# Layer 0 of a four-layer image network: how q*v is stored and how the right-hand blocks are loaded

## The chip, the cores and the metric

One core of one Trainium2 chip runs the whole network, in float32. The metric is the device time of one execution in microseconds (us). Before the change it is 5754.43 us, the median of three runs (5752.62 to 5759.0).

## What is computed

The input is 8 images of 56 x 56 pixels and 192 channels. Four layers follow one another, each as `x = x + layer(group_norm(x))`. The change lies in layer 0 alone. Cut to what matters, that layer is:

```python
p = silu(x @ p_w.T + p_b); q = silu(x @ q_w.T + q_b); v = silu(x @ v_w.T + v_b)   # 192 -> 576 channels
a1 = rpe_mlp(positions, t1) * decay      # for each channel, one coefficient for each of 111 lags
a2 = rpe_mlp(positions, t2) * decay
qv = q * v                               # (8, 56, 56, 576)
o1 = toeplitz(qv, a1)  # along a row:    o1[h, w] = sum over w' of a1[w - w'] * qv[h, w']
o2 = toeplitz(qv, a2)  # along a column: o2[h, w] = sum over h' of a2[h - h'] * qv[h', w]
out = (p * (o1 + o2)) @ o_w.T + o_b
```

For one channel, `o1 + o2` is a product of matrices, qv (56 x 56) times a Toeplitz matrix, plus another Toeplitz matrix times qv. The kernel makes one product of it: the left operand has the 56 rows of a Toeplitz matrix and the 56 rows of qv above one another in its partitions, the right operand has qv and the other Toeplitz matrix in the same order, and TensorE sums over all these partitions.

## The kernel before

Layer 0 has two stages, written one after the other from line 1320 on.

**The q*v stage** (lines 1322 to 1361) loops over the 8 images. `layer0_load` (353) fetches an image into `x0` by a transfer that GpSimd (POOL) issues. An image lies as 128 partitions, 64 channels of each half of the pixels, by 3 groups of channels by 1568 pixels (`NH`). `layer0_in` (358) takes the statistics on VectorE (DVE) at line 157 and normalizes into `xn0` on DVE at line 371, for image 0 in four pieces of 392 pixels (`TT`) and for the others in one instruction. `layer0_qv` (374) walks over the image in 14 tiles (`PH`) of 112 pixels, two image rows of each half. For each tile and each half `n` of the 576 channels TensorE (PE) does 24 matmuls at line 387, DVE adds the bias from PSUM into `act` (line 393, four buffers), ScalarE (ACT) applies SiLU in place (394), and DVE multiplies q by v into `qv` (395). The sync engine (SP) stores the tile twice: to `left`, where a row of 56 x 64 values is one image row h, with one transfer for each half of the pixels (398), and to `right`, where a row is one image column w, with two transfers for each half (403). All these stores move pieces of 256 B.

Between the tiles, lists of other steps are worked off (`between`, line 1341): `toeplitz_rows` (227) makes the coefficients and stores the Toeplitz rows to `left` and `right` from ACT's queue, 64 rows for each group of 64 channels, of which 56 hold coefficients (`row`, 295) and 8 hold zeros (`zeros`, 300). `build_bias_mask` (307) and `layer1_weights` (624) prepare layer 1; their transfers are issued by POOL.

**The mix stage** (`layer0_mix`, 523) goes through each image in three passes (`PASSES`, line 27), over nine groups of 64 channels: four, four and one. `layer0_block` (410) loads one group into two tiles of 128 partitions by 3584 values, `lt` from `left` and `rt` from `right`, with two buffers each. One transfer fills one tile: of `lt` the even partitions with a Toeplitz row and the odd ones with a row of qv, of `rt` the other way round, 64 rows of each, so the partitions past the 56th pair meet zero rows. `layer0_operand` (422) copies eight channels at a time into matmul operands, `lc` on POOL and `rc` on DVE and ACT in turn (line 425); `layer0_products` (428) multiplies them on TensorE (433) and the result is copied out (590, 593). While the products of one pass run, the gate of the pass before it (`layer0_gate`, 435, and `layer0_gate_last`, 477) is worked off in pieces. After the first pass the image before is stored to `x1` by two transfers of 64 partitions (`store`, 536), the image is normalized again (531) and the next one loaded (`load`, 526). All transfers of the mix stage go out from SP, in one order.

In both stages the order in which each engine and each queue gets its instructions is made by the framework's scheduler; no order is written out by hand there. Each engine works its instructions off in that order, so one that waits holds up all behind it.

Of the kernel before, what the change touches and what calls it, by code (L numbers as in the profile page):

```python
# [10 lines left out]
F32 = mybir.dt.float32  # L11
AF = mybir.ActivationFunctionType
# [6 lines left out]
NT = H * W  # L19
# [43 lines left out]
NH = NT // 2  # L63
NTH = NH // TT
# [25 lines left out]
def kernel(ctx: ExitStack, tc: tile.TileContext, a: dict, out: bass.AP):  # L90
# [45 lines left out]
    none = dram.tile([QR], F32, name="none")  # L136
    left, right = (dram.tile([(nimg * W + 64) * NSUB, QR], F32, name=n) for n in ("left", "right"))
    qv_row = lambda b, s: (b * NSUB + s) * W
    toep_row = lambda s: nimg * NSUB * W + 64 * s
# [87 lines left out]
    def toeplitz_rows(psum, pool, rows):  # L227
# [62 lines left out]
        zero = pool.tile([128, QR // 128], F32, name="zero", bufs=1)  # L290
        nc.gpsimd.memset(zero, 0.0)
        nc.scalar.dma_start(none.rearrange("(p n) -> p n", p=128), zero)
        parts = [z[toep_row(0):].rearrange("(s k) n -> k s n", k=64) for z in (left, right)]
# [6 lines left out]
        def zeros(i, k):  # L300
            nc.scalar.dma_start(parts[i][k], none.partition_broadcast(NSUB))

        rows += [lambda i=i, k=k: zeros(i, k) for i in range(2) for k in range(W, 64)]
# [54 lines left out]
    def layer0_in(b, x, pool, psum):  # L358

        sc, sh = scsh[:, 0, b:b + 1], scsh[:, 1, b:b + 1]  # L360
        st = pool.tile([128, 3, NTH, 6], F32, name="gh_st")
        for t in range(NTH):
            gn_piece(st, x, t)
        mv = pool.tile([128, 1, 2], F32, name="gh_mv")
        gn_aggregate(st, mv[:, 0])
        run(gn_finish(mv, sc, sh, pool, psum, "qv"))
        xn = pool.tile([128, 3, NH], F32, name="xn0")
        n = NH if b else TT
        for t in range(NH // n):
            ts = bass.ts(t, n)  # L370
            nc.vector.tensor_scalar(xn[:, :, ts], x[:, :, ts], sc, sh, ALU.mult, ALU.add)
        return xn

    def layer0_qv(b, xn, pool, psum, w_qv, b_qv, between):

        lv, rv = (
            z[qv_row(b, 0):qv_row(b, 0) + NSUB * W].rearrange("(s h) (w d) -> s h w d", h=W, d=64) for z in (left, right)
        )
        for i in range(PH):
            qv = pool.tile([2 * W, 2, D1], F32, name="qv", bufs=3)  # L380
            for n in range(2):
                ns = slice(n * D1 // 2, (n + 1) * D1 // 2)
                ps = [psum.tile([2 * W, 2, 512], F32, name=f"qv{s}", tag="qv") for s in range(2)]
                for which in range(2):
                    for j in range(3):
                        for s in range(2):
                            nc.tensor.matmul(  # L387
                                ps[s][:, which, 0:D1 // 2], xn[64 * s:64 * s + 64, j, bass.ts(i, 2 * W)],
                                w_qv[64 * s:64 * s + 64, j, which, ns], start=(j == 0), stop=(j == 2),
                            )  # L390
                for s in range(2):
                    act = pool.tile([2 * W, 2, D1 // 2], F32, name="act", bufs=4)
                    nc.vector.tensor_tensor(act, ps[s][:, :, 0:D1 // 2], b_qv[:, :, ns], ALU.add)  # L393
                    nc.scalar.activation(act, act, AF.Silu)  # L394
                    nc.vector.tensor_tensor(qv[:, s, ns], act[:, 0], act[:, 1], ALU.mult)
            for s in range(2):
                h0 = H // 2 * s + 2 * i
                nc.sync.dma_start(
                    lv[:, h0:h0 + 2].rearrange("s h w d -> (h w) s d"),
                    qv[:, s].rearrange("t (s d) -> t s d", d=64),  # L400
                )
                for r in range(2):
                    nc.sync.dma_start(
                        rv[:, :, h0 + r].rearrange("s w d -> w s d"),
                        qv[r * W:(r + 1) * W, s].rearrange("w (s d) -> w s d", d=64),
                    )
            for step in between[i]:
                step()

    def layer0_block(b, s, raws):  # L410
# [3 lines left out]
        rows_qv, rows_t = qv_row(b, s), toep_row(s)  # L414
        for t, z, even, odd in ((raw[0], left, rows_t, rows_qv), (raw[1], right, rows_qv, rows_t)):
            one = z[even:even + 64]
            nc.sync.dma_start(
                t, bass.AP(one.tensor, one.offset, [[QR, 64], [(odd - even) * QR, 2], [1, QR]]),
            )
        return raw  # L420

    def layer0_operand(copy, raw, name, bufs, d0, nu, pool):

        c = pool.tile([128, 2, 8, W], F32, name=name, bufs=bufs)
        copy(c[:, 0:nu], raw.rearrange("p (w u d) -> p u d w", u=nu, d=64 // nu)[:, :, d0:d0 + 8])  # L425
# [896 lines left out]
    with ExitStack() as st:  # L1322
# [3 lines left out]
        b_qv = pool.tile([2 * W, 2, D1], F32, name="b_qv", bufs=1)  # L1326
        nc.scalar.dma_start(b_qv.rearrange("p a d -> p (a d)"), a["b_qv"].partition_broadcast(2 * W))
# [11 lines left out]
        for b in range(nimg):  # L1339

            between = {i: [lambda i=i: pop(rows, 2 if i % 3 == 1 else 1)] for i in range(PH)}
            if b == 0:
                for i in range(PH):
# [340 lines left out]
```

## Time and profile before

| | us |
|---|---|
| median of three runs | 5754.43 |
| the profiled execution, its time | 5770.6 |
| the profiled execution, its span | 5768.8 |
| q*v stage, from the first line-387 matmul to the first products | 28 to 850 |
| mix stage | 850 to 2041 |
| TensorE busy in these two | 731 of 822 and 1072 of 1191 |
| DVE busy in these two | 601 of 822 and 646 of 1191 |
| POOL busy in these two | 45 of 822 and 550 of 1191 |
| DMA share in these two | 0.85 and 0.67 |

Times in the profile are measured from the start of the span. PE is TensorE's matmul, PEld its weight load, SPq, ACTq and POOLq are the instructions with which an engine issues transfers. The DMA share is the mean busy share of the 16 DMA engines. "Idle before, releaser" in a group's line is the time that the engine stood still just ahead of these instructions, and what it then waited for. After layer 0 come three more layers, to 5768.8 us, whose code is the same in both kernels.

### The profile page before, as it was taken

The numbers are of one execution on the slowest core, as the hardware profiler recorded it, in microseconds if no ns is written. First come the engines' busy times: TensorE is split into PE (matmuls) and PEld (weight loads), VectorE is DVE, ScalarE is ACT, GpSimd is POOL, SyncE is SP. The second block draws the span as 40 slices with busy tenths as digits, with TensorE's granted clock in tenths as the row PEclk, the third lists the DMA queues.
The fourth block names the chain that finished last, engine by engine and source line by source line (L and its number), as shares of the span: only waits on it lengthen the run. The fifth ranks groups of instructions, "written<-read, shape, count | busy, mean of one in ns | idle before, by whom it ended". The sixth has DMA issues, their size and how long they took to land. (4 is left out here: it accounts for less than half of the span.)

```text
span 5768.8 us, 116138 instructions
## 1 busy us (share of the span) xinstructions
PE 5181.2 (90%) x50342; PEld 3376.1 (59%) x50342; DVE 3336.5 (58%) x4710; ACT 2169.1 (38%) x2908; POOL 1420.2 (25%) x1107
## 2 busy tenths in 40 slices
PE   6898998999899979999997989999788798999999
PEld 4568765666666645555554657676344597444444
DVE  5777774555555546566665868888778202433331
ACT  2333443333333423333332004555476400433333
POOL 2100004444444424433342013333101101100100
PEclk8999999999999989999998989999899899999999
DMA  6888986776677633222222866666687598212211
GB/s 179 204 211 216 206 182 258 264 264 258 247 262 264 222 92 82 69 75 76 69 65 76 260 235 218 227 232 209 160 232 215 222 328 295 78 62 77 76 41 26
DMA packets 721922, 1013.94 MB, mean 176 GB/s; under 512 B 486376, under 2 KB 645444, under 8 KB 694644
## 3 DMA queue, kind: packets, MB, share of 16 engines
q1 hardware_dynamic: 706352, 940.12, 52.4%
q0 software_dynamic: 8512, 40.62, 2.1%
q10 hardware_dynamic: 6548, 25.78, 1.4%
q8 instruction: 396, 6.49, 0.5%
q14 instruction: 114, 0.93, 0.0%
HBM read 676.92 MB, written 345.97 MB: 177 GB/s over the span
## 5 line engine op out<-in xcount | busy, mean ns | idle before, releaser
L387 PE MATMUL qv<-w_qv_sb,xn 64*112 64x288 f32 x5376 | 711.3, 421 | 48.6 <-DVE act L393 45.4
L425 POOL COPY lc<-lt 128x896 f32<-128x896 f32 (+1 forms) x320 | 552.5, 1751 | 640.9 <-PE op L433 543.1
L387 PEld LDWEIGHTS qv<-w_qv_sb,xn 64*112 64x112 f32 x5376 | 558.5, 182 | 195.5 <-DVE act L393 58.1
L394 ACT ACTIVATE act<-act 112x576 f32<-112x576 f32 x448 | 300.6, 683 | 466.8 <-DVE act L393 427.4
L433 PE MATMUL op<-rc,lc 128*56 128x56 f32 x9216 | 339.1, 221 | 102.1 <-POOL lc L425 64.9
L433 PEld LDWEIGHTS op<-rc,lc 128*56 128x56 f32 x9216 | 307.8, 135 | 177.9 <-POOL lc L425 103.5
L1289 PE MATMUL ph<-y,w_sb 64*128 64x392 f32 x2304 | 397.7, 497 | 6.5 <-ACT hid L1293 6.5
L1300 PE MATMUL po<-hid,w_sb 128*64 128x392 f32 x2304 | 386.3, 494 | 0.0
L393 DVE TENSOR_TENSOR act<-qv,b_qv 112x576 f32<-112x576 f32 x448 | 320.7, 752 | 92.7 <-PE qv L387 92.4
L1307 DVE TENSOR_TENSOR x<-x,z 128x392 f32<-128x392 f32 x96 | 67.0, 698 | 524.2 <-ACT z L1305 524.2
L425 ACT COPY rc<-rt 128x896 f32<-128x896 f32 (+1 forms) x160 | 256.3, 1606 | 249.7 <-PE op L433 227.2
L805 PE MATMUL qk_ps<-xr,wg 64*96 64x392 f32 x1536 | 334.2, 538 | 1.8 <-DVE xr L752 1.7
L1016 PE MATMUL cv<-zc,wt 128*128 128x224 f32 x1536 | 313.6, 356 | 24.2 <-DMA zc<-pd 24.2
L1016 PEld LDWEIGHTS cv<-zc,wt 128*128 128x128 f32 x1536 | 291.0, 190 | 67.5 <-issue 51.2
L1289 PEld LDWEIGHTS ph<-y,w_sb 64*128 64x128 f32 x2304 | 220.0, 188 | 175.9 <-issue 25.5
L445 PE MATMUL pj<-xn,w_p_sb 64*128 64x392 f32 x1536 | 309.8, 511 | 12.4 <-DVE xn L533 8.2
L1190 PE MATMUL cps<-zc,wt 128*128 128x224 f32 x1536 | 300.2, 356 | 18.2 <-DMA zc<-zd 16.8
L1190 PEld LDWEIGHTS cps<-zc,wt 128*128 128x128 f32 x1536 | 289.6, 189 | 28.7 <-issue 21.3
L466 PE MATMUL y<-pp,w_o_sb 128*64 128x392 f32 x1536 | 285.9, 501 | 4.8 <-DVE x L474 4.1
L459 DVE TENSOR_TENSOR pp<-pp,ot 128x784 f32<-128x784 f32 x128 | 124.2, 970 | 284.8 <-ACT pp L450 272.9
L1300 PEld LDWEIGHTS po<-hid,w_sb 128*64 128x64 f32 x2304 | 162.7, 137 | 213.8 <-issue 213.8
L1031 POOL TENSOR_TENSOR rows<-rows,loc 128x896 f32<-128x896 f32 x96 | 220.8, 2300 | 261.7 <-ACT rows L1027 201.9
(233 smaller groups left out, 8895.1 us busy)
## 6 DMA issues: line engine op xcount, KB each, us to landing
lt<-left SPq DMA_DIRECT2D x72, 1792.0 KB
rt<-right SPq DMA_DIRECT2D x72, 1792.0 KB
left<-qv SPq DMA_DIRECT2D x224, 252.0 KB
right<-qv SPq DMA_DIRECT2D x448, 126.0 KB
wt<-in_band_dram SPq DMA_DIRECT2D x23, 2048.0 KB
wt<-in_band_dram SPq DMA_DIRECT2D x11, 4096.0 KB
zc<-pd SPq DMA_DIRECT2D x187, 232.0 KB
pd<-pt SPq DMA_DIRECT2D x7, 5568.0 KB
```

The costliest lines, as they stand in the source:

```text
L387: nc.tensor.matmul(ps[s][:, which, 0:D1 // 2], xn[64 * s:64 * s + 64, j, bass.ts(i, 2 * W)], w_qv[64 * s:64 * s + 64, j, which, ns], start ...
L393: nc.vector.tensor_tensor(act, ps[s][:, :, 0:D1 // 2], b_qv[:, :, ns], ALU.add)
L394: nc.scalar.activation(act, act, AF.Silu)
L425: copy(c[:, 0:nu], raw.rearrange("p (w u d) -> p u d w", u=nu, d=64 // nu)[:, :, d0:d0 + 8])
L433: nc.tensor.matmul(op[64 * u:64 * u + W, i, :], lc[:, u, i], rc[:, u, i], start=True, stop=True)
L445: nc.tensor.matmul(ps[0:M, s, 0:TT], w_p[64 * s:64 * s + 64, j, d0:d0 + M], xn[64 * s:64 * s + 64, j, ts], start=(j == 0), stop=(j == 2),)
L466: nc.tensor.matmul(y[64 * s:64 * s + 64], w_o[0:M, c, 64 * j:64 * j + 64], pp[0:M, s], start=(c == gated[0][0]), stop=(c == gated[-1][0]),)
L805: nc.tensor.matmul(in_pairs(ps[s]), wg[64 * s:64 * s + 64, j, c0:c0 + HC], in_slots(xr[64 * s:64 * s + 64], (3 * g + j) * GW), start=(j == ...
L1016: nc.tensor.matmul(dst, wt[:, c4 + i, 128 * q:128 * q + 128], zc[:, :, c4 + i, q:q + NPAIR], start=(q == 0), stop=(q == 1),)
L1190: nc.tensor.matmul(dst.rearrange("p (b n) -> p b n", n=NPAIR), wt[:, c4 + i, q * OP:(q + 1) * OP], zc[:, :, c4 + i, q:q + NPAIR], start=(q ...
L1289: nc.tensor.matmul(ps[:, s, 0:TT], w0[64 * s:64 * s + 64, j, m * 128:(m + 1) * 128], y[64 * s:64 * s + 64, j, ts], start=(j == 0), stop=(j ...
L1300: nc.tensor.matmul(ps[64 * s:64 * s + 64], w1[:, m, 64 * j:64 * j + 64], hid[:, m, s], start=(m == 0), stop=(m == 5),)
```

## The change

- Images 0, 2, 4 and 6 store q*v once, to `left` alone. Their tiles need no longer end on an image row: they are 13, twelve of 120 pixels and one of 128 (`QT`). Images 1, 3, 5 and 7 keep 14 tiles of 112 pixels and both stores. `right` holds q*v of the odd images only.
- For an even image the q*v half of `rt` is gathered from `left`: partition w gets, for each h, the 64 channels at (h, w), in pieces of 256 B.
- A block is loaded without zero rows, by four transfers of 56 rows: partitions 0 to 55 and 56 to 111 of `lt`, and the same of `rt`. The copies at line 425 and the products work on 112 partitions instead of 128. The zero rows are no longer written.
- In the q*v stage the product q times v is made on DVE for the first half of the pixels and on POOL for the second.
- Normalizing in the q*v stage is done in four pieces for every image, on DVE for image 0 and on POOL for the others.

```diff
+QT = [[(120 * i, 120) for i in range(12)] + [(1440, 128)], [(112 * i, 112) for i in range(14)]]
...
-    none = dram.tile([QR], F32, name="none")
-    left, right = (dram.tile([(nimg * W + 64) * NSUB, QR], F32, name=n) for n in ("left", "right"))
+    left, right = (dram.tile([n * NSUB, QR], F32, name=z) for n, z in ((nimg * W + 64, "left"), (nimg // 2 * W + 64, "right")))
     qv_row = lambda b, s: (b * NSUB + s) * W
-    toep_row = lambda s: nimg * NSUB * W + 64 * s
+    toep_row, right_row = (lambda s, n=n: n * NSUB * W + 64 * s for n in (nimg, nimg // 2))
...
-        rows += [lambda i=i, k=k: zeros(i, k) for i in range(2) for k in range(W, 64)]
         rows += [lambda i=i, w0=w0: row(i, w0) for i in range(2) for w0 in range(W)]
...
-        n = NH if b else TT
-        for t in range(NH // n):
-            ts = bass.ts(t, n)
-            nc.vector.tensor_scalar(xn[:, :, ts], x[:, :, ts], sc, sh, ALU.mult, ALU.add)
+        for t in range(NTH):
+            ts = bass.ts(t, TT)
+            eng = nc.gpsimd if b else nc.vector
+            eng.tensor_scalar(xn[:, :, ts], x[:, :, ts], sc, sh, ALU.mult, ALU.add)
...
-        for i in range(PH):
-            qv = pool.tile([2 * W, 2, D1], F32, name="qv", bufs=3)
+        for i, (t0, M) in enumerate(QT[b % 2]):
+            qv = pool.tile([128, 2, D1], F32, name="qv", bufs=3)
...
-                    nc.vector.tensor_tensor(qv[:, s, ns], act[:, 0], act[:, 1], ALU.mult)
+                    eng = (nc.vector, nc.gpsimd)[s]
+                    eng.tensor_tensor(qv[0:M, s, ns], act[0:M, 0], act[0:M, 1], ALU.mult)
...
                 nc.sync.dma_start(
-                    lv[:, h0:h0 + 2].rearrange("s h w d -> (h w) s d"),
-                    qv[:, s].rearrange("t (s d) -> t s d", d=64),
+                    bass.AP(one.tensor, one.offset + 64 * (NH * s + t0), [[64, M], [64 * NT, NSUB], [1, 64]]),
+                    qv[0:M, s].rearrange("t (s d) -> t s d", d=64),
                 )
-                for r in range(2):
+                for r in range(2 * (b % 2)):
                     nc.sync.dma_start(
-                        rv[:, :, h0 + r].rearrange("s w d -> w s d"),
+                        rv[:, :, H // 2 * s + 2 * i + r].rearrange("s w d -> w s d"),
                         qv[r * W:(r + 1) * W, s].rearrange("w (s d) -> w s d", d=64),
                     )
...
-        rows_qv, rows_t = qv_row(b, s), toep_row(s)
-        for t, z, even, odd in ((raw[0], left, rows_t, rows_qv), (raw[1], right, rows_qv, rows_t)):
-            one = z[even:even + 64]
+        x, at = left[qv_row(b, s):qv_row(b, s) + W], qv_row(b // 2, s)
+        nc.sync.dma_start(raw[0][0:W], left[toep_row(s):toep_row(s) + W])
+        nc.sync.dma_start(raw[0][W:2 * W], x)
+        nc.sync.dma_start(raw[1][W:2 * W], right[right_row(s):right_row(s) + W])
+        if b % 2:
+            nc.sync.dma_start(raw[1][0:W], right[at:at + W])
+        else:
             nc.sync.dma_start(
-                t, bass.AP(one.tensor, one.offset, [[QR, 64], [(odd - even) * QR, 2], [1, QR]]),
+                raw[1][0:W].rearrange("w (h d) -> w h d", d=64), x.rearrange("h (w d) -> w h d", d=64)
             )
...
-        c = pool.tile([128, 2, 8, W], F32, name=name, bufs=bufs)
-        copy(c[:, 0:nu], raw.rearrange("p (w u d) -> p u d w", u=nu, d=64 // nu)[:, :, d0:d0 + 8])
+        c = pool.tile([2 * W, 2, 8, W], F32, name=name, bufs=bufs)
+        copy(c[:, 0:nu], raw[0:2 * W].rearrange("p (w u d) -> p u d w", u=nu, d=64 // nu)[:, :, d0:d0 + 8])
```

The bias `b_qv` is loaded for 128 partitions instead of 112, and the loops over `between` run over as many tiles as the image has.

## The prediction

> **What bounds the kernel now.** I read the page first, for which engine is busy where, then the busy times by stretch over layer 0, then the sync queue's order of issue and the waits. Layer 0 has two stages. The q*v stage (line 387) runs from 28 to 850 us of the span, the mix stage (lines 410 to 621) from there to 2041 us.
>
> ```profile
> span 5768.8 us, 116138 instructions
> L387 PE MATMUL qv<-w_qv_sb,xn 64*112 64x288 f32 x5376 | 711.3, 421 | 48.6 <-DVE act L393 45.4
> L425 POOL COPY lc<-lt 128x896 f32<-128x896 f32 (+1 forms) x320 | 552.5, 1751 | 640.9 <-PE op L433 543.1
> ```
>
> In the q*v stage TensorE is busy 711.3 of 822 us with its own line alone: TensorE sets that stage. In the mix stage it is not so even. One image takes 149 us there. The columns below are: stretch, then busy us and instructions of PE, PEld, DVE, ACT, POOL, then granted clock, DMA share, GB/s.
>
> ```profile
> 1150.00:1210.00 60.00, 50.68 (x891) 33.36 (x890) 42.64 (x52) 25.79 (x25) 38.48 (x19) 0.97 0.78 265
> 1210.00:1251.00 41.00, 37.76 (x540) 25.69 (x540) 19.17 (x24) 17.66 (x17) 21.12 (x12) 1.00 0.87 360
> 1251.00:1299.00 48.00, 48.00 (x458) 31.63 (x455) 21.49 (x31) 15.07 (x17) 9.69 (x9) 1.00 0.40 154
> ...
> 1307.00:1411.00 104.00, 91.52 (x1456) 63.23 (x1454) 62.48 (x77) 44.52 (x43) 60.34 (x33) 0.98 0.88 330
> ```
>
> Each image has three passes. In the first two the DMA share is 0.78 and 0.87 and TensorE has gaps; in the third (1251:1299) TensorE is full and the DMA engines are half idle. The next image's blocks 2 to 8 and one further all fall into 1307:1411. The sync queue shows that the transfers pace this:
>
> ```profile
> 1376.90 0.51 SPq L417 DMA_DIRECT2D lt<-left  x1
> ...
> 1388.20 0.51 SPq L417 DMA_DIRECT2D lt<-left  x1
> ...
> 1399.15 0.51 SPq L417 DMA_DIRECT2D lt<-left  x1
> ```
>
> A block (lt and rt, 3.67 MB) every 11 us is what 330 GB/s gives. With two buffers each, a third pair can't be loaded ahead, so a slower block load shows in the time. Price of a block now: from the first issue of that stretch (1307.0) to the issue of the eighth (1399.2) lie seven blocks, the x1 store (2.41 MB at 203 GB/s, row below, 11.9 us) and the x load (2.41 MB at 424, 5.7): (92.2 - 17.6) / 7 = 10.7 us.
>
> The rows that the change turns on are transfers that touch only half of the partitions:
>
> ```profile
> 1044.00:1049.00 5.00, 4.35 (x76) 3.18 (x74) 4.62 (x6) 2.96 (x3) 4.85 (x3) 1.00 0.95 203
> 1050.00:1052.00 2.00, 2.00 (x19) 1.26 (x16) 0.00 (x0) 0.35 (x2) 1.83 (x2) 1.00 0.98 204
> 1061.00:1064.00 3.00, 2.84 (x26) 1.83 (x23) 0.97 (x1) 0.65 (x2) 2.95 (x2) 1.00 1.05 445
> ```
>
> The first two are the x1 store of line 538, two transfers of 64 partitions: all DMA engines are busy, and move 203 GB/s. The third is the x load of line 528, 128 partitions: 445 GB/s at 1.05, so 424 at full share. Half of the partitions, half of the pace; and the second half of the store (1050:1052), though it is queued behind the first, doesn't make it up by running beside it.
>
> **The change, part by part.**
>
> *Block loads in four transfers of 56 rows.* Removed: 72 x 2 transfers of 128 rows. Added: 72 x 4 of 56 rows, into partitions 0:56 or 56:112, so each lies nearly in one half. Bytes fall from 3.67 to 3.21 MB. The nearest row for the pace is the 203 GB/s of the x1 store. By bytes a transfer of 56 x 14336 B = 0.803 MB takes 3.95 us; but rows move whole (the stretch from 1376 to 1411 has 791 large packets for 11.3 MB, one row of 14336 B each), and 56 rows over 16 engines leave four rows on the busiest, as 64 rows do, which is 0.918 MB at 203, 4.52 us. Four transfers: 15.8 to 18.1 us. I take 17.0, between them, because engines with three rows start on the next transfer. The far bound is that nothing is lost: 3.21 MB at 330 GB/s, 9.7 us. [...]
>
> *Gathered right-hand blocks, images 0, 2, 4, 6.* One of the four transfers becomes 56 x 56 pieces of 256 B. No 256 B read is in the trace of before; the nearest row is the 256 B stores of the q*v stage, where reading and writing change places:
>
> ```profile
> 775.00:825.00 50.00, 50.00 (x416) 37.12 (x414) 40.29 (x70) 23.23 (x35) 0.00 (x0) 1.00 0.88 181
> ...
> q1 hardware_dynamic: 35708, 8.95, 87.6%
> ```
>
> 0.876 x 16 x 50 us / 35708 = 19.6 ns a piece on an engine, so 3136 pieces over 16 take 3.8 us. Upper bound: half pace again, 7.7 us. I take 4.2, near the lower end, since 256 B in 19.6 ns is 13 GB/s an engine, what the half-partition rows reach anyway (203 / 16). With three plain transfers (12.8) an even block also comes to 17.0 us; its bounds are 7.3 + 3.8 = 11.1 and 13.6 + 7.7 = 21.3.
>
> *Sum of the mix stage.* Seven blocks of an image wait in that chain: 7 x (17.0 - 10.7) = 44 us an image, 353 us over eight. The eighth block of the chain is hidden by the third pass (48 us with the DMA share at 0.40), which still covers it at 17 us. The sync queue issues 144 transfers more at 0.51 us, 74 us on a queue that mostly waits; a gather may hold it while it drains, with only block loads queued behind, which wait for the engines anyway. POOL, ACT and DVE copy 112 rows instead of 128 in the same time (their cost is by columns): nothing. Products with 112 rows instead of 128: weight loads of 56*128 (139 ns) and 128*56 (138 ns) cost the same, so nothing.
>
> *q*v tiles.* Even images run 13 tiles instead of 14. TensorE saves 711.3 / 8 / 14 = 6.35 us in each of four images, 25.4 us, on the path. Sixteen fewer bias adds (0.75 us), 232 fewer products on DVE (0.457), 7 normalizings (2.73): 137 us off DVE, which is busy 601 of 822 us, so off the path but for the stalls below. Stores to `right` vanish in four images (224 of 448, and 8 of 224 to `left`): the DMA share there falls from 0.88 toward half, and TensorE was already full at 0.88, so nothing. The 16 zero rows (0.69 us each on ACT's queue, ACT busy 322 of 822 us): nothing.
>
> *POOL's new work.* 216 products: the nearest row is line 1031, 2300 ns for 896 columns, so 0.74 us for 288; 28 normalizings of 1176 columns at 1.95 (line 425) to 2.57 ns a column, 2.3 to 3.0 us. Together 225 to 245 us of 822, where POOL was busy 45. POOL works in order, and now a product stands behind POOL's transfers:
>
> ```profile
> POOL x L355 <- DVE xn L371: 360.6, 5, 105.0
> POOL w_p_sb L109 <- PE qv L387: 311.3, 1, 311.3
> POOL bmask L346 <- DVE bmt L342: 52.7, 8, 22.8
> POOL wgd L669 <- DVE w_qkv_sb L666: 49.5, 1, 49.5
> ...
> DVE gh_st L157 <- DMA x<-in_x_dram: 40.3, 6, 7.7
> ```
>
> Who waits for a late product: its store, then one of the four `act` buffers, then line 393 on DVE, then TensorE. The 52.7 and 49.5 us could be held against TensorE: at worst all 102 us, with 25 saved by the tiles, +77. On the other side the 40.3 us that DVE waits for x, which come from loads released by the old normalizing, may shrink: at best -65. I take -25, the tiles alone, nearer the middle.
>
> *Total.* The profiled execution took 5770.6 us, 16.2 above the median of the three runs. 5770.6 + 353 - 25 = 6098.6; against the median 5754.4 + 328 = 6082 us.
>
> **Rivals.** *No loss of pace (faster than before).* If the hardware spreads 56 rows so that no two engines meet on one half, an odd block takes 9.7 and an even one 11.1 us, mean 10.4: 56 x (10.4 - 10.7) = -17, with the tiles -25: 5712 us. It decides at a mean block time of 10.7 + 25 / 56 = 11.1 us; below that the kernel is faster. For it: fewer bytes. Against it: 203 GB/s in both halves of the x1 store. Chance 0.15.
>
> *Engines drift apart*, so that half of the time one works in the lower and its partner in the upper partitions: 13 us a block, 56 x 2.3 = +129, 5858 us. For it: four transfers in a row alternate halves. Against: 1050:1052. Chance 0.14.
>
> *The gather is the bound*: even blocks 21.3, odd ones 17.0: 28 x 10.6 + 28 x 6.3 = +473, 6203 us. Chance 0.10.
>
> **How the numbers follow.** The forecast (0.61) is 6082; its own range, from 15.8 to 18.1 us a block (+286, +414) and -65 to +77 in the q*v stage, is 5975 to 6245. The range 5800 to 6250 leaves out the fast rival and little else. A difference under 0.2% (11.5 us) can't be told from none here. Faster 0.12, same 0.03 (the fast rival with some POOL stalls), slower 0.85.
>
> **What would show it.** Right: in the mix stage an image takes about 193 us instead of 149, the issues of lt in the second pass stand 17 us apart, the stage moves near 190 to 200 GB/s at a high DMA share, and waits of POOL, DVE and ACT line 425 for lt and rt grow from 89 us to some hundreds, while the third pass stays at 48 us. q*v: even images 6 us shorter than odd ones. Wrong: lt issues still 11 us apart, or TensorE in the q*v stage waiting for act behind POOL's products.

## The result, and the profile after

The changed kernel takes 6126.5 us (median of 4 runs, 6116.0 to 6129.6) against 5756.7 us (4 runs on the same chip) for the kernel before: ratio 1.0638, 95% interval 1.0619 to 1.0656. It is slower by 370 us, 44 us above the forecast of 6082 and inside its range. The profiled execution took 6126.92 us, 356.3 more than the one of before.

The page of the changed kernel (line 423 was 425, 381 was 387, 431 was 433):

```profile
span 6125.1 us, 115683 instructions
...
L423 POOL COPY lc<-lt 112x896 f32<-112x896 f32 (+1 forms) x320 | 518.7, 1651 | 1062.2 <-PE op L431 958.1
L381 PE MATMUL qv<-w_qv_sb,xn 64*112 64x288 f32 (+2 forms) x5184 | 691.9, 425 | 50.6 <-DVE act L387 46.3
...
L431 PE MATMUL op<-rc,lc 112*56 112x56 f32 x9216 | 390.4, 247 | 233.6 <-DVE rc L423 136.2
...
L390 POOL TENSOR_TENSOR qv<-act 112x288 f32<-112x288 f32 (+2 forms) x216 | 173.1, 802 | 507.3 <-ACT act L388 425.3
```

TensorE's line of the q*v stage has become 19.4 us cheaper, and the idle time before it is as small as it was (50.6 us, 48.6 before). POOL's copies of the blocks now follow 1062.2 us of idle time instead of 640.9: the work behind the block loads is what waits.

Where the 356 us lie can be read from the first and last matmul of each stage in the two traces. The q*v stage ran from 28.6 to 846.7 us and now runs from 26.2 to 828.8: 15.5 us shorter, and it starts 2.4 us earlier. The mix stage (first to last matmul of line 433, now 431) ran from 854.4 to 2052.5 and now runs from 835.5 to 2425.2, all counted from start to start: 1589.7 instead of 1198.1, 391.6 us longer. What follows the mix stage takes 3699.9 instead of 3716.3, though none of its code changed. With 1.1 us less between the two stages, these give 391.6 - 15.5 - 2.4 - 1.1 - 16.4 = 356.2.

Busy time by stretch, after. The columns are: stretch, length, busy us and instructions of PE, PEld, DVE, ACT, POOL, then granted clock, DMA share, GB/s. The first line is the q*v stage, the second the mix stage, and the last three follow one another inside it; 1296:1352 has the same gate work (96 matmuls each of lines 443 and 464) as 1251:1299 of before, which the prediction called the third pass. Below them stands the mix stage of the kernel before.

```profile
28.00:830.00 802.00, 710.76 (x5318) 570.64 (x5314) 475.59 (x869) 298.10 (x451) 250.70 (x316) 0.92 0.70 161
840.00:2415.00 1575.00, 1233.82 (x14764) 802.85 (x14762) 623.38 (x804) 455.91 (x459) 512.79 (x318) 0.85 0.80 167
1251.00:1296.00 45.00, 31.08 (x476) 23.47 (x472) 21.74 (x28) 15.94 (x15) 20.66 (x12) 0.72 0.94 173
1296.00:1352.00 56.00, 51.51 (x420) 28.37 (x422) 18.85 (x25) 13.19 (x13) 6.90 (x4) 0.95 0.97 204
1352.00:1459.00 107.00, 80.91 (x1128) 57.19 (x1127) 41.37 (x58) 33.19 (x35) 42.82 (x28) 0.82 0.78 157
```

```profile
860.00:2040.00 1180.00, 1066.91 (x14713) 716.09 (x14713) 638.80 (x801) 461.38 (x458) 544.47 (x316) 0.98 0.67 250
```

The mix stage moves fewer bytes than before at a higher DMA share: 167 GB/s at 0.80, against 250 at 0.67. In 1251:1296 the engines are nearly full and move 173 GB/s; where before 330 GB/s were moved at 0.88, TensorE now does 31 us of work in 45. The third pass, which had the DMA share at 0.40, now has it at 0.97 and takes 56 us instead of 48. The granted clock, 0.97 to 1.00 in the image shown of before, is 0.72 and 0.82 in the stretches where TensorE has gaps.

The sync queue, after, at the issue of a block's first transfer; an image with gathered blocks first, then one without:

```profile
1260.63 0.91 SPq L409 DMA_DIRECT2D lt<-left  x1
...
1280.71 0.31 SPq L409 DMA_DIRECT2D lt<-left  x1
...
1300.38 2.56 SPq L409 DMA_DIRECT2D lt<-left  x1
...
1562.43 0.31 SPq L409 DMA_DIRECT2D lt<-left  x1
...
1581.22 0.31 SPq L409 DMA_DIRECT2D lt<-left  x1
```

The 11 us between these blocks have become 20.1, 19.7 and 18.8. The distances are uneven, and these are three of them: in the first of the two images others are 16.9, 20.9, 35.3 and 9.5 us, and the store of x1 is issued within the 19.7. So the regular 17 us that the prediction named is not seen, and the time of a whole image is the surer measure. The groups of waits of the engines that copy from lt and rt, before and then after, and those of the sync queue after:

```profile
POOL lc L425 <- DMA lt<-left: 62.7, 14, 11.1
...
DVE rc L425 <- DMA rt<-right: 15.4, 8, 5.7
...
ACT rc L425 <- DMA rt<-right: 11.0, 7, 2.2
```

```profile
POOL lc L423 <- DMA lt<-left: 99.0, 27, 9.3
...
DVE rc L423 <- DMA rt<-left: 82.2, 10, 15.1
...
ACT rc L423 <- DMA rt<-left: 61.1, 8, 12.4
...
DVE rc L423 <- DMA rt<-right: 44.3, 4, 12.8
...
ACT rc L423 <- DMA rt<-right: 37.2, 4, 11.2
```

```profile
SPq L409 <- POOL lc L423: 1183.2, 66, 33.8
```

The five lines of after add up to 324 us of waiting for blocks, the three of before to 89. The rows tell the same: in the packets of the mix stage, a row of 14336 B took 535 ns in the median before and 1093 ns after, and a 256 B piece, which is in this stage the gather, 32 ns (mean 33).

The packets also tell how many are under way at one time. In 1307:1411 of the kernel before, 16 or more are, for 72% of the time. In 1562:1581 of the changed kernel, where only transfers of 56 rows run, it is 14 for 84% of the time and 15 for nearly all the rest, at a DMA share of 0.88, which is 14 of 16.

### The profile page after: what moved, and what is told of

It is laid out like the page before. It is cut to its first block, busy times and chain, and to the rows that moved or that the text cites. A ratio compares the mean times of both kernels' runs of the same rounds, so it can differ in the third digit from the quotient of the medians.

```text
span 6125.1 us, 115683 instructions
## 1 busy us (share of the span) xinstructions
PE 5317.9 (87%) x50150; PEld 3456.6 (56%) x50150; DVE 3203.6 (52%) x4455; ACT 2140.1 (35%) x2892; POOL 1596.2 (26%) x1350
## 5 line engine op out<-in xcount | busy, mean ns | idle before, releaser
L423 POOL COPY lc<-lt 112x896 f32<-112x896 f32 (+1 forms) x320 | 518.7, 1651 | 1062.2 <-PE op L431 958.1
L381 PE MATMUL qv<-w_qv_sb,xn 64*112 64x288 f32 (+2 forms) x5184 | 691.9, 425 | 50.6 <-DVE act L387 46.3
L381 PEld LDWEIGHTS qv<-w_qv_sb,xn 64*112 64x112 f32 (+2 forms) x5184 | 555.2, 187 | 180.9 <-DVE act L387 56.9
L431 PE MATMUL op<-rc,lc 112*56 112x56 f32 x9216 | 390.4, 247 | 233.6 <-DVE rc L423 136.2
L431 PEld LDWEIGHTS op<-rc,lc 112*56 112x56 f32 x9216 | 357.3, 160 | 292.4 <-issue 172.0
L388 ACT ACTIVATE act<-act 112x576 f32<-112x576 f32 (+2 forms) x432 | 279.6, 683 | 468.3 <-DVE act L387 437.0
L387 DVE TENSOR_TENSOR act<-qv,b_qv 112x576 f32<-112x576 f32 (+2 forms) x432 | 307.7, 751 | 210.3 <-PE qv L381 209.0
L423 ACT COPY rc<-rt 112x896 f32<-112x896 f32 (+1 forms) x160 | 256.6, 1609 | 284.4 <-PE op L431 167.6
L1014 PEld LDWEIGHTS cv<-zc,wt 128*128 128x128 f32 x1536 | 290.9, 190 | 66.3 <-issue 50.2
L448 ACT ACTIVATE pp<-pj,vecs_sb 128x784 f32<-128x784 f32 x128 | 117.0, 914 | 595.0 <-PE pj L443 436.7
L390 POOL TENSOR_TENSOR qv<-act 112x288 f32<-112x288 f32 (+2 forms) x216 | 173.1, 802 | 507.3 <-ACT act L388 425.3
```

The costliest lines, as they stand in the source:

```text
L381: nc.tensor.matmul(ps[s][0:M, which, 0:D1 // 2], xn[64 * s:64 * s + 64, j, t0:t0 + M], w_qv[64 * s:64 * s + 64, j, which, ns], start=(j == ...
L387: nc.vector.tensor_tensor(act[0:M], ps[s][0:M, :, 0:D1 // 2], b_qv[0:M, :, ns], ALU.add)
L388: nc.scalar.activation(act[0:M], act[0:M], AF.Silu)
L423: copy(c[:, 0:nu], raw[0:2 * W].rearrange("p (w u d) -> p u d w", u=nu, d=64 // nu)[:, :, d0:d0 + 8])
L431: nc.tensor.matmul(op[64 * u:64 * u + W, i, :], lc[:, u, i], rc[:, u, i], start=True, stop=True)
L1014: nc.tensor.matmul(dst, wt[:, c4 + i, 128 * q:128 * q + 128], zc[:, :, c4 + i, q:q + NPAIR], start=(q == 0), stop=(q == 1),)
```

## The experiments

Three things are bundled in the slower mix stage: fewer partitions per transfer, more transfers in another order, and the gather. A fourth, POOL's work, lies in the q*v stage. My theory was that a transfer that reaches only half of the partitions goes at half the pace. The rivals were that 56 rows use too few DMA engines, that more transfers or the engines' order of work cost the time, that the gather does, and that POOL does. Periods below are the mean of the seven distances between the eight images' normalizings in the mix stage: 151.4 us before, 201.2 after. In the changed kernel the seven alternate between 188 us and 207 to 215; the longer ones hold most of the gathered blocks.

**Four transfers of 56 rows alone**, in the kernel before, with zero rows, gathers and POOL's work left as they were:

```diff
-        for t, z, even, odd in ((raw[0], left, rows_t, rows_qv), (raw[1], right, rows_qv, rows_t)):
-            one = z[even:even + 64]
-            nc.sync.dma_start(
-                t, bass.AP(one.tensor, one.offset, [[QR, 64], [(odd - even) * QR, 2], [1, QR]]),
-            )
+        nc.sync.dma_start(raw[0][0:W], left[rows_t:rows_t + W])
+        nc.sync.dma_start(raw[0][W:2 * W], left[rows_qv:rows_qv + W])
+        nc.sync.dma_start(raw[1][W:2 * W], right[rows_t:rows_t + W])
+        nc.sync.dma_start(raw[1][0:W], right[rows_qv:rows_qv + W])
...
-        c = pool.tile([128, 2, 8, W], F32, name=name, bufs=bufs)
+        c = pool.tile([2 * W, 2, 8, W], F32, name=name, bufs=bufs)
```

> The kernel before, with its block loads alone changed: four transfers of 56 rows for each block, operands of 112 partitions; no gather, no POOL products, 14 tiles everywhere. Theory H (a transfer that touches only half of the partitions goes at half pace): rows of 14336 B take near 1.07 us instead of 0.535, a block 17 to 18 us instead of 10.7, 7 x (17.5 - 10.7) x 8 = +381 us, so 6100 to 6150 us, and an image takes about 195 us in the mix stage. Rival G (the gather costs the time): under 100 us above before, 5760 to 5850 us.

6108.6 us, ratio 1.0607 (1.0575 to 1.0638). Its mix stage by stretch:

```profile
860.00:2370.00 1510.00, 1189.28 (x14722) 767.21 (x14719) 639.36 (x802) 456.20 (x458) 526.13 (x315) 0.89 0.75 174
```

This part alone makes nearly the whole loss. The period is 193.4 us, 42.0 more than before; over the seven blocks of the chain that is 6.0 us more on 10.7, so a block costs 16.7 where the prediction took 17.0. Rows take 1088 ns in the median, and in 1300:1420 14 packets are under way for 60% of the time. My estimate from these, four rows on each of 14 engines, four transfers long, is 17.4 us at that pace; at the 535 ns of before it would be 8.6, less than the 10.7 of before.

**Two transfers of 64 rows per tile.** Is it the half span, or that 56 is not a multiple of 16? Here all the bytes of before are loaded, each half of a tile by its own transfer:

```diff
-        for t, z, even, odd in ((raw[0], left, rows_t, rows_qv), (raw[1], right, rows_qv, rows_t)):
-            one = z[even:even + 64]
-            nc.sync.dma_start(
-                t, bass.AP(one.tensor, one.offset, [[QR, 64], [(odd - even) * QR, 2], [1, QR]]),
-            )
+        nc.sync.dma_start(raw[0][0:64], left[rows_t:rows_t + 64])
+        nc.sync.dma_start(raw[0][64:128], left[rows_qv:rows_qv + 64])
+        nc.sync.dma_start(raw[1][64:128], right[rows_t:rows_t + 64])
+        nc.sync.dma_start(raw[1][0:64], right[rows_qv:rows_qv + 64])
```

> The kernel before, with each 128-row transfer of a block split into two of 64 rows, Toeplitz rows in one half of the partitions and q*v rows in the other; same bytes, zero rows kept, 128-partition operands. Theory H (half of the partitions): four rows on each of 16 engines at half pace, 16 x 1.07 = 17.1 us a block, as slow as the 56-row version, 6080 to 6150 us, DMA share near 0.97 while it loads. Rival E (56 rows leave two of 16 engines idle or spread badly, and that is the cause): 64 rows divide by 16, so within 40 us of before, 5720 to 5800 us.

6120.1 us, ratio 1.0630 (1.0598 to 1.0661), rows 1120 ns, period 194.4:

```profile
866.00:2390.00 1524.00, 1182.69 (x14744) 753.98 (x14744) 631.23 (x802) 456.91 (x459) 530.32 (x316) 0.90 0.87 194
```

The engines are busy 0.87 of the whole stage and move 194 GB/s. In 1300:1420 16 packets or more are under way for 80% of the time. 64 rows gain nothing over 56, so the loss isn't one of too few engines. TensorE's order has changed here and in the kernel with 56 rows (from the first product to the last it changes 322 and 320 times between products and other matmuls, 570 before), so these two don't yet part the pace from the order.

**One transfer of 112 rows per tile**, which reaches both halves, interleaved as before, with an eighth fewer bytes:

```diff
-                t, bass.AP(one.tensor, one.offset, [[QR, 64], [(odd - even) * QR, 2], [1, QR]]),
+                t[0:2 * W], bass.AP(one.tensor, one.offset, [[QR, W], [(odd - even) * QR, 2], [1, QR]]),
...
-        c = pool.tile([128, 2, 8, W], F32, name=name, bufs=bufs)
+        c = pool.tile([2 * W, 2, 8, W], F32, name=name, bufs=bufs)
```

> The kernel before, with each 128-row transfer cut to 112 rows in one transfer, Toeplitz and q*v rows interleaved as before, so that the transfer spans 112 partitions; bytes down by an eighth. Theory H in its plain form (only the half span hurts): 3.21 MB at 330 GB/s, 9.7 us a block or less, at or below before, 5690 to 5760 us. Theory H with pairs (each engine takes a run of neighbouring rows, and engines meet on the same part of the partitions whenever the transfer is not the full 128): as slow as the 56-row version, 6000 to 6150 us.

6051.8 us, ratio 1.0505 (1.0473 to 1.0538), rows 1047 ns, period 189.8:

```profile
860.00:2340.00 1480.00, 1179.05 (x14738) 788.27 (x14735) 601.40 (x802) 461.56 (x459) 513.15 (x317) 0.87 0.76 178
```

Here the number of transfers and the sync queue's order are those of before, TensorE's matmuls stand in the same order but for 14 places of 50342, and the time still rises by some 295 us. So the pace is enough, with no change of order. But the form of my theory falls: it isn't only the half span that is slow. 112 of 128 partitions are as slow as 56. Again 14 packets are under way most of the time (64% of 1300:1420). By my estimate, eight rows on each of 14 engines in each of two transfers, a block is 16.8 us at 1047 ns and 8.6 at 535, so it is the pace of each row that is lost, and not the two engines. Half the pace for half of the partitions, which the prediction read off the x1 store (203 beside 424 GB/s), fits 56 rows (1088 ns) and 64 (1120 ns) and does not by itself say why 112 rows should take 1047 ns. Whether the rows' other division over 14 engines does it, no run shows.

**Twice the transfers, all of them over 128 partitions**, each loading half of the columns. Is it the number of transfers?

```diff
-            nc.sync.dma_start(
-                t, bass.AP(one.tensor, one.offset, [[QR, 64], [(odd - even) * QR, 2], [1, QR]]),
-            )
+            for c in range(0, QR, QR // 2):
+                nc.sync.dma_start(
+                    t[:, c:c + QR // 2],
+                    bass.AP(one.tensor, one.offset + c, [[QR, 64], [(odd - even) * QR, 2], [1, QR // 2]]),
+                )
```

> The kernel before, with each 128-row transfer split into two over its columns: 128 partitions by 7168 B each. Four transfers a block, as in the 56-row and 64-row versions, but all partitions in each. The scheduler makes another order of the engines from this one too. Theory H (the pace of part-partition transfers is the cause): rows go at near 26 GB/s an engine, a block in 10.7 to 11.5 us, 5740 to 5810 us. Rival O (four transfers a block instead of two, all behind one release, and the order of the engines that the scheduler makes from them, are the cause): 6000 us or more with a low DMA share, as in the version with 64 rows in the middle partitions, where the DMA engines stood idle for 31% of the stage.

5763.6 us, ratio 1.0012 (1.0000 to 1.0023):

```profile
860.00:2040.00 1180.00, 1054.92 (x14628) 708.15 (x14630) 638.31 (x797) 459.12 (x455) 536.56 (x315) 0.98 0.68 250
```

Four transfers a block on the sync queue, issued in another order than before, cost nothing that counts: 250 GB/s at 0.68, where the stage of before has 250 at 0.67. TensorE's order, though, is near that of before (566 changes), so this run parts the number of transfers from the pace, and not a much changed order of TensorE.

**Another place for the 64 rows.** If rows that meet in one half share what is scarce, 64 rows in partitions 32 to 95, a quarter of the tile on each side of the middle, should run at full pace:

```diff
-        for t, z, even, odd in ((raw[0], left, rows_t, rows_qv), (raw[1], right, rows_qv, rows_t)):
-            one = z[even:even + 64]
-            nc.sync.dma_start(
-                t, bass.AP(one.tensor, one.offset, [[QR, 64], [(odd - even) * QR, 2], [1, QR]]),
-            )
+        for t, z, mid, ends in ((raw[0], left, rows_t, rows_qv), (raw[1], right, rows_qv, rows_t)):
+            nc.sync.dma_start(t[32:96], z[mid:mid + 64])
+            nc.sync.dma_start(t[0:32], z[ends:ends + 32])
+            nc.sync.dma_start(t[96:128], z[ends + 32:ends + 64])
```

This puts the rows of lt and rt at other partitions than the products expect, alike in both, and a sum over partitions is the same.

> The kernel before, with the 64 + 64 rows of each tile placed otherwise: one set in partitions 32 to 95 by one transfer, the other in 0 to 31 and 96 to 127 by two of 32 rows; same bytes and rows as in the version with two transfers of 64 rows, 6120 us. Theory H with pairs (each engine takes a run of neighbouring rows; two engines whose partitions lie 32 apart in one half share a way into SBUF): the middle set has no such pair, 4 rows of 0.535 us, the two others go at half pace, 2 x 2 rows of 1.07: 6.4 us a tile, 12.8 a block instead of 17.1, so 7 x 4.3 x 8 = 240 us faster than 6120, near 5880, and of the 14336 B rows half take 0.535 us. Rival (whatever is not one transfer of 128 rows is slow, or more transfers cost more): 6100 us or above, few rows of 0.535.

6155.4 us, ratio 1.0691 (1.0677 to 1.0706): a miss, the slowest of all. The rows did speed up: 535 ns for the fastest twentieth, 586 for the first quarter, 949 in the median, 867 in the mean against 1084 with two times 64 rows. The stage did not:

```profile
860.00:2440.00 1580.00, 1178.48 (x14700) 771.89 (x14701) 622.23 (x801) 452.43 (x457) 508.53 (x315) 0.89 0.69 187
```

```profile
SPq L416 <- POOL lc L424: 1049.4, 69, 30.6
```

The block issued at 1441.12 us, with no row under way just before it, shows the pace by itself: its rows landed between 1442.4 and 1455.8, 13.4 us, near the 12.8 expected. Most rows of its 64-row transfers took 535 to 600 ns, those of the 32-row transfers behind them mostly 950 to 1110. But the blocks around it were issued 39.2 and 26.7 us apart. The engines are idle for 31% of the stage, and the sync queue waits 1049 us for POOL to free lt, about as long as with two times 64 rows (1037). All six transfers of a block stand behind that one release, and TensorE's order is another (212 changes between products and other matmuls, 322 with two times 64 rows). Whether that order makes the time, or six transfers behind one release, no run tells apart. So where rows lie goes with their pace, but pace does not explain this kernel's time. Which engine takes which row, and what two engines share, no run shows; shown is the time of a row by the partitions it goes to.

**The gather taken out**, in the changed kernel: even images load 56 plain rows of `left` where they gathered. This leaves out the exchange of rows and columns, so their results are not those of the network.

```diff
-            nc.sync.dma_start(
-                raw[1][0:W].rearrange("w (h d) -> w h d", d=64), x.rearrange("h (w d) -> w h d", d=64)
-            )
+            nc.sync.dma_start(raw[1][0:W], x)
```

> The changed kernel, with the gather of the even images replaced by a plain load of the same 56 rows of left, so the q*v half of rt holds rows where columns are wanted. In the changed kernel's mix stage a 256 B piece takes 33 ns, 224 on an engine 7.4 us, against 4 rows of 1.09 us = 4.4: if the gather is dearer by that, 3.0 us x 7 blocks x 4 images = 84 us faster than the changed kernel, about 6040 us. If the gather hides in the idle time of the engines: as the changed kernel, 6126 us within 15. If the gather is the whole loss: near 5750 us.

6083.1 us, ratio 1.0561 (1.0530 to 1.0591), period 192.7:

```profile
850.00:2360.00 1510.00, 1187.27 (x14696) 758.73 (x14693) 643.78 (x805) 454.67 (x457) 527.45 (x316) 0.91 0.75 174
```

It lies 43 us below the changed kernel by the medians; the two intervals leave 16 to 73. The gather costs that much, not nothing and not the whole. By its pieces: 3136 x 33 ns / 16 = 6.5 us an engine, against 16.7 / 4 = 4.2 for a plain transfer of 56 rows, so 2.3 us a block and 28 x 2.3 = 64 us if none were hidden. This divides by 16 engines; over 14 it would be 7.4 us. From the first piece to the last a gather took 6.7 to 9.2 us, partly beside other transfers.

**POOL's work taken back to DVE**, in the changed kernel, and **given to POOL** in the kernel before:

```diff
-            eng = nc.gpsimd if b else nc.vector
+            eng = nc.vector
...
-                    eng = (nc.vector, nc.gpsimd)[s]
+                    eng = nc.vector
```

> The changed kernel, with all products and all normalizing of the q*v stage on DVE again. If POOL's share of the work is what made the q*v stage 16 us shorter: 10 to 20 us slower than the changed kernel, 6135 to 6150. If the 13 tiles of the even images did it and POOL is neutral: within 10 us of 6126. If POOL's products hold TensorE up: faster than 6115.

```diff
-        n = NH if b else TT
-        for t in range(NH // n):
-            ts = bass.ts(t, n)
-            nc.vector.tensor_scalar(xn[:, :, ts], x[:, :, ts], sc, sh, ALU.mult, ALU.add)
+        for t in range(NTH):
+            ts = bass.ts(t, TT)
+            eng = nc.gpsimd if b else nc.vector
+            eng.tensor_scalar(xn[:, :, ts], x[:, :, ts], sc, sh, ALU.mult, ALU.add)
...
-                    nc.vector.tensor_tensor(qv[:, s, ns], act[:, 0], act[:, 1], ALU.mult)
+                    eng = (nc.vector, nc.gpsimd)[s]
+                    eng.tensor_tensor(qv[:, s, ns], act[:, 0], act[:, 1], ALU.mult)
```

> The kernel before, with half of the products of the q*v stage and the normalizing of images 1 to 7 on POOL and nothing else changed. In the changed kernel the q*v stage of the odd images is as long as before (within 1.5 us each), so POOL's work should be neutral: 5745 to 5765 us. If DVE's 125 us freed shorten the stage: 5710 to 5740. If POOL's waits hold TensorE up: above 5775.

Back on DVE: 6117.3 us, ratio 1.0621 (1.0602 to 1.0640), which can't be told from the changed kernel's 1.0638. Its q*v stage ran from 26.6 to 820.7 us, 794.2, against 802.6 after and 818.1 before. So the thirteen tiles alone save 23.9 us in these traces, and POOL's part gives 8.4 of it back. These are single traces, and the stage varies: in the seven kernels that have its code of before it took 817 to 826 us. With thirteen tiles it took 803 and 805 us with POOL's part and 794 and 792 without. On POOL in the kernel before: 5777.5 us, ratio 1.0038 (1.0024 to 1.0052), slower by 21 us, with a q*v stage of 829.1 us, 11.0 longer. The waits of that kernel fit this:

```profile
POOL qv L396 <- DMA right<-qv: 123.3, 53, 6.8
...
PE qv L387 <- DVE act L393: 59.3, 17, 10.3
```

POOL's product waits 53 times for the stores that still read the qv buffer, and TensorE waits 59.3 us for DVE's bias add instead of 45.4. In the changed kernel, whose even images store nothing to `right`, POOL waits 50.2 us for these stores.

**The old 128-row loads kept, with the thirteen tiles and the gather**, on DVE. Even images load the right-hand tile in two interleaved transfers of 56 rows, one of them the gather; all else is 128 rows (the zero rows come back for it):

```diff
...
-        nc.sync.dma_start(raw[0][0:W], left[toep_row(s):toep_row(s) + W])
-        nc.sync.dma_start(raw[0][W:2 * W], x)
-        nc.sync.dma_start(raw[1][W:2 * W], right[right_row(s):right_row(s) + W])
+        def pairs(t, z, even, odd):
+            one = z[even:even + 64]
+            nc.sync.dma_start(t, bass.AP(one.tensor, one.offset, [[QR, 64], [(odd - even) * QR, 2], [1, QR]]))
+
+        pairs(raw[0], left, toep_row(s), qv_row(b, s))
         if b % 2:
-            nc.sync.dma_start(raw[1][0:W], right[at:at + W])
+            pairs(raw[1], right, qv_row(b // 2, s), right_row(s))
         else:
+            x = left[qv_row(b, s):qv_row(b, s) + W]
+            nc.sync.dma_start(raw[1][1:2 * W:2], right[right_row(s):right_row(s) + W])
             nc.sync.dma_start(
-                raw[1][0:W].rearrange("w (h d) -> w h d", d=64), x.rearrange("h (w d) -> w h d", d=64)
+                raw[1][0:2 * W:2].rearrange("w (h d) -> w h d", d=64), x.rearrange("h (w d) -> w h d", d=64)
             )
```

> The changed kernel's q*v stage (13 tiles in even images, q*v stored once there) without POOL's work, with zero rows and transfers of 128 rows again wherever the data allow it: all lt, and rt of the odd images. In even images rt comes by a 56-row transfer and the gather, each into every second partition. Theory H: the q*v stage 24 us shorter than before; an even block takes 4.3 (lt) + 4.3 (56 rows at half pace) + 7.4 (224 pieces of 33 ns), 16 us instead of 10.7, 7 x 5.3 x 4 = +148 us: about 5880 us. If the order of the engines is a cause of its own, above 5950. If the gather costs little at all: under 5780.

5856.9 us, ratio 1.0167 (1.0150 to 1.0184). Two neighbouring images by stretch:

```profile
1034.00:1183.00 149.00, 136.20 (x1853) 91.21 (x1851) 80.68 (x103) 56.29 (x57) 62.95 (x38) 0.98 0.74 234
1183.00:1377.00 194.00, 155.21 (x1920) 99.84 (x1916) 82.22 (x106) 59.56 (x60) 73.18 (x43) 0.89 0.72 202
```

Periods alternate between 145 to 149 and 191 to 195. Where the loads are of 128 rows the period of before is back, with the thirteen tiles' saving kept (q*v stage 792 us). The periods with gathered blocks still pay some 45 us each. Gather and 56-row transfer come together here, so their shares stay open. Loading the right-hand tile of even images in this way does not pay even with 128-row loads elsewhere: the mix stage is 154 us longer than before (1352.3 against 1198.1), and what the q*v stage saves is 26.

**The old kernel's own half transfers made whole.** The store of x1 was two transfers of 64 partitions. Here x1 is kept in DRAM as the tile lies, is stored in one transfer, and is read back accordingly:

```diff
-    x1 = [dram.tile([C, NT], F32, name=f"x1_{b}") for b in range(nimg)]
+    x1 = [dram.tile([128, 3 * NH], F32, name=f"x1_{b}") for b in range(nimg)]
...
-            for s in range(2):
-                nc.sync.dma_start(
-                    x1[b].rearrange("(j p) n -> p j n", p=64)[:, :, s * NH:(s + 1) * NH], x[64 * s:64 * s + 64]
-                )
+            nc.sync.dma_start(x1[b], x.rearrange("p j n -> p (j n)"))
...
+        if not store:
+            d = dram_image.rearrange("p (j h w) -> p j h w", j=3, w=W)
+            for s in range(2):
+                for h0, h1 in ((21, 25), (25, 28)) if g == 3 else ((g0, g0 + 7),):
+                    p0, r0 = 64 * ((s + (h0 + 3) // 28) % 2), (h0 + 3) % 28
+                    queues[s % len(queues)].dma_start(
+                        tile_image[64 * s:64 * s + 64, :, h0:h1], d[p0:p0 + 64, :, r0:r0 + h1 - h0]
+                    )
+            return
```

> The kernel before, with x1 kept in DRAM in the layout of the SBUF tile, so that its store is one transfer of 128 partitions instead of two of 64, and layer 1's shifted loads read it in that layout. If the half-partition pace is what makes this store 12 us, it takes 5.7 us instead, 6.2 us less in each image's chain of loads: 7 x 6.2 = 43 us faster than before, 5715 us; half of it, 5735, if the chain has slack there. If the pace has another cause (the direction, the row size of 6272 B): as before, 5745 to 5765.

5730.0 us, ratio 0.9952 (0.9940 to 0.9964): faster than both kernels, by 26 us against the one before, where 43 were expected or 21 with slack in the chain. The stretch of one such store, issued at 1187.0 us, with the first rows of the next block at its end:

```profile
1187.00:1195.00 8.00, 6.31 (x124) 4.87 (x124) 8.00 (x10) 5.03 (x4) 6.76 (x4) 1.00 0.93 353
```

353 GB/s where the two halves moved 203, and the period falls from 151.4 to 148.6 us. So a transfer of half the partitions, taken out of the kernel before, gives time back. Its rows grew as well, from 6272 to 18816 B, and no run parts that from the span; pieces of 7168 B over 128 partitions took 272 ns in the kernel with twice the transfers, 26 GB/s an engine, but those were loads.

## Why the prediction was right, and where its terms were off

- *Half the pace, in the mix stage: right.* The term was 353 us. Four transfers of 56 rows alone lengthen the mix stage by 330.2 us (1528.3 against 1198.1) and the period by 42.0 where 44 was taken. Three things in its reasoning were not. It made the half span the cause, and 112 rows over both halves are as slow. It took 17.0 because engines with three rows would start early, which no run shows; the 14 packets under way fit 14 engines of four rows each instead, 17.4 us, so that the number came so near is partly luck. And it expected the third pass to stay at 48 us and hide the eighth block; in the stretch shown the DMA engines are full there too, and it takes 56. The 190 to 200 GB/s that it named as a sign were 167, and 174 with four transfers of 56 rows alone.
- *The number of engines.* The prediction spread 56 rows over 16 engines; four rows on the busiest were the upper end of its range, 18.1 us a block, and 5754.4 + 414 - 25 = 6143 us in all. The changed kernel came nearer to that than to 6082, with 14 packets under way for 84% of 1562:1581, where 64 rows have 16 or more for 80% of 1300:1420. But the two missing engines are not what costs the time: two times 64 rows, which 16 divides, take as long (6120.1 us). The packets don't name their engine, so how the rows are shared out no run shows.
- *The gather: too cheap.* Priced at 4.2 us, as much as a plain transfer; its pieces took 33 ns where those of the 256 B stores took 19.6, so 6.5 us over 16 engines and 7.4 over 14. Both stay within the bound of 7.7. The experiment without it puts 43 us on it in the whole; in the two traces the mix stage is 60.4 longer with it (1589.7 against 1529.3). With this the mix stage's 391.6 us come within reach: 330.2 + 60.4 = 390.6.
- *Steps counted as nothing.* With 112 rows instead of 128 the copies of 896 columns took 1802 ns instead of 1936 on POOL, 1356 instead of 1424 on DVE and 1770 instead of 1764 on ACT. The products took 247 ns instead of 221 and their weight loads 160 instead of 135, in a stage with a granted clock of 0.85 instead of 0.98. The issue of a gather took the sync queue 0.54 us in the median and 1.33 at most, but the two issues of the x1 store, where they stand right behind a gather, took 17.67, 16.09 and 15.58 us, against 1.24 to 1.33 behind plain loads: there the queue was held, and with it more than block loads.
- *The thirteen tiles: right.* 25.4 us predicted, 23.9 measured with POOL's part taken out, in a stage that varies by up to 9 us between traces.
- *POOL's work: its two ends held, its value of nothing did not.* In the two traces it costs 8.4 us of the q*v stage, about as much as the stage varies by. Its product took 802 ns where 740 was worked out, its normalizing 1333 where 2300 to 3000 was. The wait named, POOL's transfers held up by DVE with a product behind them, shrank from 52.7 and 49.5 us to 25.7 and 2.3; seen instead is that POOL waits for the stores out of qv, as in the kernel before with POOL's work added.
- *Not foreseen.* Where the blocks are late the granted clock falls, to 0.85 in the mix stage, and PE's busy time there rises from 1066.9 us in 1180 to 1233.8 in 1575 for nearly the same instructions (14713 and 14764). How much of the loss this is, beside the waiting that comes with it, no run tells apart.
- *The rest of the kernel*, 16.4 us shorter, wasn't in the sum. It was 3716.9 us in the kernel with four transfers of 56 rows, 3699.9 without the gather, 3705.3 with 112 rows and 3678.5 with 128-row loads and the gather, with the same code behind the mix stage; so it moves without a change to its code, and why is open. Against the sum, then: mix +38.6, q*v and start 6 less saved than taken, this -16.4: 28 us above 6098.6, the profiled 6126.9.

The rival of no lost pace falls with the first experiment. The rival of engines that drift apart would have given 13 us a block; measured are 16.7, and that engines work in pairs no run shows. The rival in which the gather is the bound gave 21.3 us a gathered block; 20.1 and 19.7 are seen in one image, but the longer periods of the changed kernel, 207 to 215 us, give (207 - 151.4) / 7 + 10.7 = 18.6 to 19.8 by the working above, though they hold some plain blocks as well, and 6203 us is well above.

## What to carry to other kernels

Look at the number of partitions of a transfer before its bytes: on these traces 128 rows took 535 ns each and 112, 64 or 56 rows about 1050 to 1120 (64 rows in the middle partitions, 32 to 95, mostly 535 to 600), so loading zero rows was cheaper than leaving them out. Dropping work on one engine is worth only what its stage waits for: 24 us in the q*v stage here, where the stage that the transfers pace lost 330. Where a profile has one line of full DMA engines at half the usual GB/s, as the x1 store was, try that transfer in one piece over all partitions.

## What the runs showed that was not expected

- A 112-row transfer over both halves is as slow per row (1047 ns) as 56 rows in one half (1088); an eighth fewer bytes cost 5%.
- Transfers of 56 and of 112 rows have 14 packets under way most of the time, those of 64 and of 128 rows 16; at the pace of before, 8.6 us a block by the estimate above, the two missing would have cost nothing here.
- With 64 of the rows in partitions 32 to 95 and the others outside, a twentieth of the rows takes 535 ns again (901 with two times 64), and the kernel is still the slowest, 6155 us, with the DMA share at 0.69.
- 256 B pieces that are read from DRAM into a tile took 32 ns, those stored from a tile 18 in the median (19.6 in the q*v stage by the prediction's working).
- The granted clock was 0.59 in this stretch of the changed kernel, in which PE waits for a block and is busy 6.9 of 19 us, at 186 GB/s and a DMA share of 0.88:

```profile
1562.00:1581.00 19.00, 6.92 (x140) 6.51 (x136) 3.01 (x4) 4.47 (x4) 7.00 (x5) 0.59 0.88 186
```
